# Tying first products to their places in the text on TensorE, and one more step ahead of the resized spectra's product

## The chip, the core and the metric

The kernel runs on one core of one Trainium2 chip. The core has five engines that run their own streams of instructions and meet through semaphores: TensorE (PE in the profile; its weight loads are PEld), VectorE (DVE), ScalarE (ACT), GpSimd (POOL) and SyncE (SP), which here only issues transfers. The metric is the device time of one execution in microseconds (us); lower is better.

## What is computed

Two layers are run one after the other on 32 images of 96 channels and 56 x 56 pixels, all in float32. Cut to what matters:

```python
# layer 0: expand, depthwise 3x3, squeeze and excite, project, residual
h = silu(bn(conv1x1(x, fake_quant(w1))))            # 96 -> 576 channels
h = silu(bn(depthwise3x3(h, fake_quant(w2))))
s = sigmoid(se_w2 @ silu(se_w1 @ mean(h) + b1) + b2)
x = x + bn(conv1x1(h * s, fake_quant(w3)))          # 576 -> 96

# layer 1
mag = abs(rfft2(x))                                 # first spectrum
fe  = mag.mean(channels)
ca  = sigmoid(mlp(pooled(separable_conv7(mag))))    # a gate for each channel
s   = [x.mean(channels), sqrt((x*x).mean(channels) + 1e-6), resize(fe)]
sa  = sigmoid(conv(relu(conv(separable_conv15(s)))))# a gate for each pixel
y   = x * ca * sa
freq_e = resize(abs(rfft2(y)).mean(channels))       # second spectrum
aux = [y, coord, freq_e]
offset, gate = conv3x3(aux), sigmoid(conv(relu(conv3x3(aux))))
y_def = deformable_conv3x3(y, offset)
z = (1 - gate) * conv3x3(y) + gate * y_def
x = relu(batchnorm(z) + x)                          # statistics over all images
```

A two-dimensional transform is done as two sets of matrix products, one along rows and one along columns, and the resize of its mean over channels as one more product.

## The kernel before

**Bands and slots.** The main loop (`layers`) goes over bands: 7 bands of 8 rows in each image. A band is cut into two halves of 7 tiles. A slot is one call of `pump()`: one for each of the 14 tiles and three at the end of a band, so 17 slots a band and 119 an image. The band's own work, in the text's order, is: the weights' loads for a coming half (`prepare`, on the SP queue), the joint convolution of the band after next (L605, in `find`), the products of three tiles (L721), three slots, the end of the previous half (its deformable product L740, the multiplication of loaded weights L692, the transposes L707 of a coming half with the copy L709), the products of four tiles, four slots, and the copies L732 that pack the half. The second half is the same; three slots close the band.

**Two streams beside it.** While the bands of image b run, `pump()` also advances two generators. The first does layer 0 of image b+2 (`hidden`: products L168, SiLU L172, nine depthwise taps L261 on VectorE, SiLU L221, a store of the result to `h2d` in memory). The second does `attend` for image b+1. Both start with the sixth band of an image (`turn`), and a generator runs from one `yield` to the next at each step. How many steps are due follows from the slot:

```python
            for st in streams:
                due = st[2] * min(1.0, (slot - st[3]) / (st[4] - st[3]))
                while st[1] < due:
                    st[1] += 1
                    next(st[0], None)
```

For the second stream `st[2]` is `n_second`, the number of its steps, which is counted while the first image is prepared: 61. With slots counted from the start of the stretch, `st[3]` is 3 and `st[4]` is 111, so that the 61 steps are spread evenly over 108 slots. One further piece, after the last `yield`, runs when the stretch is drained.

**The second stream's steps**, in order, which the change touches:

1. `squeeze` (L284, L290), with loads of `hq`, the stored hidden rows (`project_loads`, L305). Four rounds of `project` follow, four steps each. A round multiplies in two halves (L323, and L329 for the chunk that both share). `hq` has one buffer for each half, so a round's load starts when the products of the round before have read the buffer. ScalarE scales the result (L333), POOL adds the residual (L466) and stores it to `x1d` (L467).
2. `dft_mag` without a gate: three loads of `x2` (L361), then six groups (row products L386; squares L370 and copies L393 on ScalarE; sums L372 on VectorE; each group's step also issues the load three groups on), then three steps of column products (L410, with squares L413 on ScalarE and sums L414 on VectorE), then a root (L417).
3. `resized_spectrum` for `fe`: the reduction L427 on VectorE, a step's end, then the product L430 and a copy L432. After it come `edge` and the small products of the channel gate and the pixel gate (L501 to L556).
4. `dft_mag` with the pixel gate: the same, but POOL multiplies each group by the gate first (`weigh`, L366), two groups ahead. There are no squares L370 and no sums.
5. `resized_spectrum` for `fy`: multiplication L426, reduction L427, a step's end, L430 and L432; then L572, and at the drain the store of `fq`, which the next image's bands read.

**What sets the order.** SP issues its transfers exactly in the order of the text (`manual_schedule`). On the other engines a planner orders the instructions by its own estimate of when each is ready, with the text's order as the priority: an instruction can run ahead of earlier ones that the planner takes to be not ready. Once ordered, an engine works its instructions off one after the other. `keep_in_program_order` ties an instruction behind the one that the text emitted just before it on the same engine. The kernel uses it once, for ScalarE's L670.

**Buffers.** Products go to banks of `mm` (six, given out in turn by `bank`), `acc` (one) and `pd` (one). A bank comes free when its reader on ScalarE or VectorE is done. `sq`, `ht`, `ybl` and each half of `hq` have one buffer.

Of the kernel before, what the change touches and what calls it, by code (L numbers as in the profile page):

```python
# [16 lines left out]
C, H, W = 96, 56, 56  # L17
# [7 lines left out]
V = W // 2 + 1  # L25
# [8 lines left out]
EW = ER * W  # L34
# [67 lines left out]
def bn_affine(nc, pool, g, b, m, v, tag):  # L102

    shape = list(g.shape)
    std = pool.tile(shape, FP, name=f"std_{tag}")
    nc.vector.tensor_scalar(std, v, EPS, None, ALU.add)
    nc.scalar.activation(std, std, AF.Sqrt)  # L107
    nc.vector.reciprocal(std, std)
    inv = pool.tile(shape, FP, name=f"bninv_{tag}")
    nc.vector.tensor_tensor(inv, g, std, ALU.mult)  # L110
    sh = pool.tile(shape, FP, name=f"bnsh_{tag}")
    nc.vector.tensor_tensor(sh, m, inv, ALU.mult)
    nc.vector.tensor_tensor(sh, b, sh, ALU.subtract)
    return inv, sh


def bank(p):
    return p["mm"].tile([128, 512], FP, name="mm")


def hidden_constants(tc, ctx, a, p):

    nc = tc.nc
    cp = ctx.enter_context(tc.tile_pool(name="l0c", bufs=1))
    w = p["w0"] = {}
    for name, shape in (("w1", [C, HID]), ("w2", [128, NCH, 9]), ("w3", [128, NCH, C])):
        w[name] = cp.tile(shape, FP, name=name)
        nc.sync.dma_start(w[name], a[name + "L"])
    for name in ("sew1", "seb1", "sew2", "seb2"):
        w[name] = cp.tile(list(a[name].shape), FP, name=name)  # L130
        nc.scalar.dma_start(w[name], a[name])
    for name, parts in (("w1", C), ("w2", 128), ("w3", 128)):
        with tc.tile_pool(name=f"fq{name}", bufs=1) as tp:
            fake_quant(nc, tp, w[name], parts, name)
    with tc.tile_pool(name="l0v", bufs=1) as tp:
        vec = tp.tile([128, 8, NCH], FP, name="vec")
        nc.scalar.dma_start(vec, a["hidvec"])
        vec3 = tp.tile([C, 4], FP, name="vec3")
        nc.scalar.dma_start(vec3, a["bn3"])
        for n, v in ((1, vec[:, :4]), (2, vec[:, 4:]), (3, vec3.unsqueeze(2))):  # L140
            inv, sh = bn_affine(nc, tp, v[:, 0], v[:, 1], v[:, 2], v[:, 3], n)
            for key, t in ((f"inv{n}", inv), (f"sh{n}", sh)):
                w[key] = cp.tile(list(t.shape), FP, name=key)
                nc.vector.tensor_copy(w[key], t)

    p["hp"] = [cp.tile([128, HH + 2, WP], FP, name=f"hp{i}") for i in range(2)]
    for t in p["hp"]:
        nc.gpsimd.memset(t, 0.0)
    p["n_hp"] = 0
# [165 lines left out]
def project(nc, p, rows):  # L315

    w, w3s = p["w0"], p["w3scaled"]
    pts = []
    for half in range(2):
        pts.append(bank(p))  # L320
        mine = [(ch, hq) for ch, hq in rows[half] if ch < NCH - 1]
        for i, (ch, hq) in enumerate(mine):
            nc.tensor.matmul(pts[half][:C, :EW], w3s[:, ch], hq, start=(i == 0), stop=False)  # L323
        if half == 0:
            yield
    (_, both), = [r for r in rows[1] if r[0] == NCH - 1]
    for half in range(2):
        ps = slice(64 * half, 64 * half + 64)
        nc.tensor.matmul(pts[half][:C, :EW], w3s[ps, NCH - 1], both[ps], start=False, stop=True)  # L329
    outs = []  # L330
    for half in range(2):
        o = p["o"].tile([C, EW], FP, name="o")
        nc.scalar.activation(o, pts[half][:C, :EW], AF.Identity, bias=w["sh3"], scale=w["inv3"])  # L333
        outs.append(o)
    yield outs


def dft_mag(nc, p, src, gate=None):

    w = p["w"]
    hwc = src.rearrange("c (h w) -> h c w", h=H)
    s1 = p["s1p"].tile([2 * WX, NP, 2 * V], FP, name="s1")  # L350
    if gate is None:
        parts = p["sq"].tile([2 * WX, 2, NPB * V], FP, name="sq")[: 2 * H, :, : NG * W].rearrange("p k (g w) -> p k g w", g=NG)
    x2s = []

    def load(g):
        if g < NG:
            x2 = p["x2"][p["n_x2"] % len(p["x2"])]
            p["n_x2"] += 1
            for half in range(2):
                c0 = half * C // 2 + g * CG  # L360
                nc.sync.dma_start(x2[half * H : (half + 1) * H, :, :W], hwc[:, c0 : c0 + CG])  # L361
            x2s.append(x2)

    def weigh(g):
        if gate is not None and g < NG:
            nc.gpsimd.tensor_tensor(x2s[g][:, :, :W], x2s[g][:, :, :W], gate.unsqueeze(1).to_broadcast([2 * H, CG, W]), ALU.mult)  # L366

    def sums(g):
        sq = bank(p)[: 2 * H, : CG * W].rearrange("h (c w) -> h c w", c=CG)
        nc.scalar.activation(sq, x2s[g][:, :, :W], AF.Square)  # L370
        for k, t in enumerate((x2s[g][:, :, :W], sq)):
            nc.vector.tensor_reduce(parts[:, k, g], t.rearrange("h c w -> h w c"), AX.X, ALU.add)  # L372

    for g in range(3):
        load(g)
    for _ in range(2):
        yield
    weigh(0)
    weigh(1)
    yield  # L380
    if gate is not None:
        yield
    for g in range(NG):
        pt = bank(p)
        for i in range(CG // 2):
            nc.tensor.matmul(pt[:, i * 4 * V : (i + 1) * 4 * V],  # L386
                             x2s[g][:, 2 * i : 2 * i + 2, :].rearrange("h c w -> h (c w)"), w["FU"],
                             start=True, stop=True)
        if gate is None:
            sums(g)  # L390
        weigh(g + 2)
        load(g + 3)
        nc.scalar.copy(s1.rearrange("p (h q) u -> p h q u", h=2)[:, :, g * CG // 2 : (g + 1) * CG // 2],  # L393
                       pt[:, : 2 * CG * V].rearrange("p (q h u) -> p h q u", h=2, u=2 * V))
        yield
    if gate is None:
        p["sums"] = p["sp"].tile([2 * H, 2, W], FP, name="sums")
        nc.vector.tensor_reduce(p["sums"], parts.rearrange("p k g w -> p k w g"), AX.X, ALU.add)
    mag = s1[:, :, :V]
    n = NQB * V  # L400
    pairs = mag.rearrange("p (r q) u -> p r q u", r=2)
    for q0 in range(0, NP // 2, NQB):
        sq = p["sq"].tile([2 * WX, 2, 2, n], FP, name="sq")
        pts = bank(p), bank(p)
        for part, first, second in ((0, (0, 0), (1, V)), (1, (0, V), (2, 0))):
            for t, (g, u0) in enumerate((first, second)):
                for r, k in ((0, 0), (1, 1), (0, 1), (1, 0)):
                    rows = slice(r * WX, r * WX + W)
                    q1 = k * NP // 2 + q0
                    nc.tensor.matmul(pts[r][k * WX : (k + 1) * WX, part * n : (part + 1) * n].rearrange("p (q u) -> p q u", q=NQB),  # L410
                                     w["GV"][rows, g], s1[rows, q1 : q1 + NQB, u0 : u0 + V], start=(t == 0), stop=(t == 1))
        for r, pt in enumerate(pts):
            nc.scalar.activation(sq[:, r].rearrange("p k n -> p (k n)"), pt[:, : 2 * n], AF.Square)  # L413
        nc.vector.tensor_tensor(pairs[:, :, q0 : q0 + NQB], sq[:, :, 0].rearrange("p r (q u) -> p r q u", q=NQB),  # L414
                                sq[:, :, 1].rearrange("p r (q u) -> p r q u", q=NQB), ALU.add)
        yield
    nc.scalar.activation(mag, mag, AF.Sqrt)  # L417
    p["magnitude"] = mag


def resized_spectrum(nc, p, mag, name, scale=None):


    m2 = p["sp"].tile([2 * WX, V], FP, name=f"m_{name}")
    if scale is not None:
        nc.vector.tensor_tensor(mag, mag, scale.unsqueeze(2).to_broadcast([2 * WX, NP, V]), ALU.mult)  # L426
    nc.vector.tensor_reduce(m2, mag.rearrange("p q u -> p u q"), AX.X, ALU.add)  # L427
    yield
    pf = p["acc"].tile([128, 512], FP, name="acc")
    nc.tensor.matmul(pf[:V, : 2 * W], m2, p["w"]["RT2"], start=True, stop=True)  # L430
    rs = p["sp"].tile([V, 2, W], FP, name=name)
    nc.scalar.copy(rs.rearrange("p m w -> p (m w)"), pf[:V, : 2 * W])  # L432
    p["resized"] = rs
    yield


def attend(tc, p, b, x, h2d, pooled, x1, given=False):
# [32 lines left out]


    yield from dft_mag(nc, p, x1)
    mag = p["magnitude"]

# [89 lines left out]


    yield from dft_mag(nc, p, x1, sa)
    yield
    yield from resized_spectrum(nc, p, p["magnitude"], "fy", cx)
    fy = p["resized"]
    pz = p["acc"].tile([128, 512], FP, name="acc")  # L570
# [929 lines left out]
```

## Time and profile before

| | |
|---|---|
| three runs, us | 9,635.6, 9,640.8, 9,673.78; median 9,640.8 |
| the profiled execution, us | 9,648.5, of which its span is 9,646.7 |
| mean granted clock of TensorE | 0.923 of full speed |
| product L323, idle time before it | 127.4 us, of which 125.9 for hq |
| product L386, idle time before it | 52.4 us: 34.3 for POOL, 17.9 for x's loads |
| product L430 on fe's sums, idle time before it | 43.1 us |
| product L430 on fy's sums, idle time before it | 43.5 us |
| multiplication L692, idle time before it on VectorE | 704.2 us, of which 690.5 for the weights' loads |

The profile is of one execution. "Busy" is the time in which an engine works, "idle before" the time in which it stood still just before the instructions of a group, with what ended most of it (written after the arrow). The granted clock is what the chip's throttle allows TensorE; at 0.5 the same product takes about twice as long. The chain that ended last, which the page follows back from the end, lies in the last 280 us (`normalise`), where images are loaded, scaled and stored; the bands end at about 9,365 us.

### The profile page before, as it was taken

The page shows a single profiled execution, that of the slowest core. Times are in us where ns is not written, and L with a number is a line of the kernel's source. Part 1 is how long each engine was busy: PE and PEld are TensorE (multiplying, and loading weights), DVE is VectorE, ACT ScalarE, POOL GpSimd, SP SyncE. Part 2 cuts the span into 40 slices and gives each one's busy share as a digit, 9 for nine tenths or more (in the row PEclk, how much of TensorE's full clock was granted, in tenths as well). Part 3 has the DMA queues.
Part 4 walks back from the last instruction along what each step waited for, and adds up shares of the span by engine and source line. Part 5 has one row for each costly group of instructions (what it writes and reads, how often), then busy time and mean ns, then how long its engine had stood idle before and what let it go on. Part 6 is the DMA issues. An engine that isn't in the chain of part 4 may idle for free. (4 is left out here: it accounts for less than half of the span.)

```text
span 9646.7 us, 129705 instructions
## 1 busy us (share of the span) xinstructions
PE 8472.7 (88%) x48374; PEld 5064.2 (52%) x48374; DVE 7227.2 (75%) x6948; ACT 5322.1 (55%) x10262; POOL 2532.6 (26%) x2642
## 2 busy tenths in 40 slices
PE   6889989998999999999899989999999999999870
PEld 3455555555555555555555555555555555555540
DVE  7688777778777787877777887777878777777323
ACT  2355555565555556555555655555555555565453
POOL 1123223222222322222232322233222323322210
PEclk9899999999999999999999999999999999999985
DMA  2355555555555555555555555555555555554449
GB/s 94 95 143 148 151 152 160 150 149 143 147 155 154 160 154 145 145 149 155 154 160 155 145 142 153 151 158 154 153 139 145 150 157 157 153 152 135 130 154 417
DMA packets 1069473, 1485.98 MB, mean 154 GB/s; under 512 B 590438, under 2 KB 840086, under 8 KB 1056550
## 3 DMA queue, kind: packets, MB, share of 16 engines
q1 hardware_dynamic: 858747, 985.20, 37.9%
q10 hardware_dynamic: 153803, 329.80, 9.2%
q0 software_dynamic: 56288, 162.60, 6.7%
q8 instruction: 388, 6.36, 0.3%
q14 instruction: 247, 2.02, 0.1%
HBM read 1064.29 MB, written 412.65 MB: 153 GB/s over the span
## 5 line engine op out<-in xcount | busy, mean ns | idle before, releaser
L261 DVE SCALAR_TENSOR_TENSOR acch<-hp,w,acch 128x1512 f32<-128x1512 f32 (+1 forms) x2250 | 4320.5, 1920 | 32.8
L605 PE MATMUL mm<-yp,c_jointW 104*128 104x448 f32 x4032 | 1649.0, 561 | 9.0 <-ACT yt L709 5.5
L740 PE MATMUL pd<-v,c_def 128*96 128x224 f32 (+1 forms) x6272 | 1414.8, 376 | 127.6 <-ACT v L732 104.1
L703 POOL COPY ybl<-yp 96x448 f32<-96x448 f32 x896 | 1014.7, 1159 | 1903.7 <-PE mm L707 1903.3
L721 PE MATMUL mm<-wc,yt 64*96 64x144 f32 x12544 | 1168.1, 308 | 153.5 <-DVE yb L638 76.8
L740 PEld LDWEIGHTS pd<-v,c_def 128*96 128x96 f32 (+1 forms) x6272 | 1051.8, 173 | 437.4 <-ACT v L732 142.5
L168 PE MATMUL mm<-xt,w 96*128 96x392 f32 (+3 forms) x2688 | 1136.3, 561 | 133.8 <-ACT yt L709 96.0
L605 PEld LDWEIGHTS mm<-yp,c_jointW 104*128 104x128 f32 x4032 | 783.6, 196 | 806.0 <-issue 762.6
L721 PEld LDWEIGHTS mm<-wc,yt 64*96 64x96 f32 x12544 | 884.2, 167 | 489.8 <-issue 188.0
L221 ACT ACTIVATE acch<-acch,sh,inv 128x1568 f32<-128x1568 f32 x288 | 487.5, 1693 | 1159.0 <-DVE acch L261 1143.9
L692 DVE TENSOR_TENSOR wc<-wc,wr 128x1008 f32<-128x1008 f32 x448 | 564.6, 1260 | 704.2 <-DMA wr<-hd 690.5
L725 ACT COPY v<-mm 96x288 f32<-96x288 f32 (+1 forms) x2688 | 1003.6, 442 | 117.7 <-PE mm L721 78.9
L172 ACT ACTIVATE hp<-mm,sh,inv 128x392 f32<-128x392 f32 (+2 forms) x1216 | 811.8, 672 | 326.9 <-PE mm L168 282.1
L633 PE MATMUL mm<-yp,c_base0W 96*64 96x448 f32 x4032 | 913.5, 550 | 0.0
L323 PE MATMUL mm<-hq,w3s 128*96 128x392 f32 x2048 | 788.2, 531 | 127.4 <-DMA hq<-h2d 125.9
L655 POOL DMA_DIRECT2D od<-at x224 | 186.3, 832 | 2275.1 <-DVE at L651 1451.9
L732 ACT COPY v<-v 32x448 f32<-32x448 f32 x1344 | 755.3, 562 | 30.3
L168 PEld LDWEIGHTS mm<-xt,w 96*128 96x128 f32 (+1 forms) x2688 | 389.9, 189 | 495.1 <-issue 264.8
L709 ACT COPY yt<-mm 128x384 f32<-128x384 f32 (+1 forms) x896 | 350.9, 441 | 491.5 <-PE mm L707 489.4
L323 PEld LDWEIGHTS mm<-hq,w3s 128*96 128x96 f32 x2048 | 336.3, 173 | 477.7 <-issue 382.5
L466 POOL TENSOR_TENSOR o<-o,xc 96x392 f32<-96x392 f32 x256 | 396.5, 1549 | 643.9 <-ACT o L333 642.3
L633 PEld LDWEIGHTS mm<-yp,c_base0W 96*64 96x64 f32 x4032 | 294.6, 134 | 515.5 <-issue 490.2
(194 smaller groups left out, 9023.7 us busy)
## 6 DMA issues: line engine op xcount, KB each, us to landing
h2d<-acch ACTq DMA_DIRECT2D x288, 784.0 KB
wc<-hd SPq DMA_DIRECT2D x896, 252.0 KB
wr<-hd SPq DMA_DIRECT2D x896, 252.0 KB
hq<-h2d SPq DMA_DIRECT2D x128, 980.0 KB
hq<-h2d SPq DMA_DIRECT2D x128, 784.0 KB
x<-x1d SPq DMA_DIRECT2D x768, 98.0 KB
ht<-od SPq DMA_DIRECT2D x224, 252.0 KB
hd<-ht ACTq DMA_DIRECT2D x224, 252.0 KB
```

What stands on the lines that cost most here:

```text
L168: nc.tensor.matmul(pt[p0 : p0 + w1.shape[1], : rows * W], w1, xts[hf][:, r0 * W : (r0 + rows) * W], start=True, stop=True)
L172: nc.scalar.activation(h1[lo:hi, row0 : row0 + rows, 1 : 1 + W], pt[lo:hi, : rows * W].rearrange("p (h w) -> p h w", h=rows), AF.Silu, bia ...
L261: nc.vector.scalar_tensor_tensor(acc[:, lo:hi], win, wk, acc[:, lo:hi], ALU.mult, ALU.add)
L323: nc.tensor.matmul(pts[half][:C, :EW], w3s[:, ch], hq, start=(i == 0), stop=False)
L605: nc.tensor.matmul(view, weights[:, k], yp[:channels, r0 : r0 + RB, dx + PD - 1 : dx + PD - 1 + W], start=(k == 0), stop=(k == NTAP - 1))
L633: nc.tensor.matmul(pb[k % 2 * BC : (k % 2 + 1) * BC, :BW].rearrange("p (h w) -> p h w", h=RB), w["base"][:, k], yp[:C, r0 : r0 + RB, dx + ...
L692: nc.vector.tensor_tensor(wc, wc, wr, ALU.mult)
L703: nc.gpsimd.tensor_copy(yb[:, :, s], blocks)
L721: nc.tensor.matmul(pt[k][:C, (t - lo) * KP : (t - lo + 1) * KP], yt[ps, t], s[ps, t * KP : (t + 1) * KP], start=True, stop=True)
L725: nc.scalar.copy(v[:C, :, lo:hi, k].rearrange("c k t p -> c t k p"), pt[k][:C, : (hi - lo) * KP].rearrange("c (t k p) -> c t k p", t=hi - ...
L732: nc.scalar.copy(v[C:, 1 + 2 * i : 3 + 2 * i], v[i * QC : (i + 1) * QC, KA:])
L740: nc.tensor.matmul(out.rearrange("c q (t x) -> c t q x", x=TS), p["w"]["def"][ks, k], v[ks, k].rearrange("c t s (r x) -> c t (s r) x", r=T ...
```

## The change

Three first products are tied: the first of each half of `project` (L323), the first of each group of the second, gated row transform (L386) and the product of each resized spectrum (L430). The helper `pinned` makes the tie if the pools' dictionary holds the context, as it does in the main loop. In `resized_spectrum` one more `yield` stands between the reduction and the product, so that a step passes between them; it is met twice in an image.

```diff
+def pinned(p, ins):
+    if "tc" in p:
+        p["tc"].keep_in_program_order(ins)
+
@@ project
         for i, (ch, hq) in enumerate(mine):
-            nc.tensor.matmul(pts[half][:C, :EW], w3s[:, ch], hq, start=(i == 0), stop=False)
+            ins = nc.tensor.matmul(pts[half][:C, :EW], w3s[:, ch], hq, start=(i == 0), stop=False)
+            if i == 0:
+                pinned(p, ins)
@@ dft_mag
         for i in range(CG // 2):
-            nc.tensor.matmul(pt[:, i * 4 * V : (i + 1) * 4 * V],
-                             x2s[g][:, 2 * i : 2 * i + 2, :].rearrange("h c w -> h (c w)"), w["FU"],
-                             start=True, stop=True)
+            ins = nc.tensor.matmul(pt[:, i * 4 * V : (i + 1) * 4 * V],
+                                   x2s[g][:, 2 * i : 2 * i + 2, :].rearrange("h c w -> h (c w)"), w["FU"],
+                                   start=True, stop=True)
+            if i == 0 and gate is not None:
+                pinned(p, ins)
@@ resized_spectrum
     nc.vector.tensor_reduce(m2, mag.rearrange("p q u -> p u q"), AX.X, ALU.add)
     yield
+    yield
     pf = p["acc"].tile([128, 512], FP, name="acc")
-    nc.tensor.matmul(pf[:V, : 2 * W], m2, p["w"]["RT2"], start=True, stop=True)
+    pinned(p, nc.tensor.matmul(pf[:V, : 2 * W], m2, p["w"]["RT2"], start=True, stop=True))
```

`n_second` is counted from the generator itself and so counts the two new steps. Nothing else in the kernel is edited, and what is computed stays the same.

## The prediction

> **What bounds the kernel now.** I read the page first: how full each engine is, and the granted clock of TensorE (PE) by slice.
>
> ```profile
> PE 8472.7 (88%) x48374; PEld 5064.2 (52%) x48374; DVE 7227.2 (75%) x6948; ACT 5322.1 (55%) x10262; POOL 2532.6 (26%) x2642
> PEclk9899999999999999999999999999999999999985
> ```
>
> TensorE is busy for 8,364.6 of the 9,165 us from 200 to 9,365 us. The last 280 us are the normalisation, which the page's chain ends on and which the change does not touch. So what counts is where TensorE stands idle. That is the view of its waits; the columns are who waits, for whom, us in total, times, longest.
>
> ```profile
> PE mm L323 <- DMA hq<-h2d: 125.9, 31, 9.4
> PE mm L168 <- ACT yt L709: 96.0, 44, 5.2
> PE mm L707 <- ACT sq L413: 80.3, 21, 6.5
> PE acc L430 <- DVE m_fe L427: 43.1, 31, 4.2
> PE acc L430 <- DVE m_fy L427: 40.0, 30, 2.9
> PE mm L386 <- POOL x L366: 34.3, 32, 4.0
> ```
>
> Some 30 times each means once an image: the stalls sit at fixed places of an image's 119 slots. An image takes 282.7 us (L430 at 856.9 and 1,139.6 us), a slot 2.4 us. So the third view is the instructions in order of time of one image. Around the first L430:
>
> ```profile
> 4240.81 1.21 DVE L692 TENSOR_TENSOR wc<-wc,wr 128x1008 f32<-128x1008 f32 x1 [4.86 <-DMA wr<-hd]
> ...
> 4242.67 1.00 ACT L413 ACTIVATE sq<-mm 128x464 f32<-128x464 f32 x2 [4.73 <-DVE s L414]
> 4243.28 0.47 PE L707 MATMUL mm<-c_ident,ybl 96*128 96x96 f32 x3 [1.12 <-ACT sq L413]
> ...
> 4246.43 1.41 ACT L417 ACTIVATE s<-s 128x1392 f32<-128x1392 f32 x1
> 4247.74 0.77 ACT L709 COPY yt<-mm 128x384 f32<-128x384 f32 x2
> 4248.26 0.93 PE L168 MATMUL mm<-xt,w 96*128 96x392 f32 x2 [2.03 <-ACT yt L709]
> ...
> 4248.39 2.54 DVE L427 TENSOR_REDUCE m_fe<-s 128x29 f32<-128x1392 f32 x1
> ...
> 4251.09 0.55 PE L430 MATMUL acc<-c_RT,m_fe 128*29 128x112 f32 x2 [1.90 <-DVE m_fe L427]
> 4251.56 1.68 PE L168 MATMUL mm<-xt,w 96*128 96x392 f32 x2
> ```
>
> It is one knot. DVE waits 4.86 us for weights, so its L414 is late, so ScalarE's square L413 is late, so a bank is not free for L707; then the root L417 is late, the copy L709 behind it, and the reduction L427 ends 0.16 us before L430 starts. Three stalls of 5.05 us in all. The last row is a product pair that takes 0.93 us at 4,248.26 and 1.68 here: the clock has halved, from 4,249.5 to 4,256.3 us (third column before the end is the granted clock):
>
> ```profile
> 4249.50:4256.30 6.80, 5.21 (x9) 2.65 (x10) 6.80 (x7) 6.27 (x12) 0.00 (x0) 0.50 0.14 38
> ```
>
> **The three ties.** A tie makes a product issue after the one that the text emits just before it on TensorE; it adds no wait and does not hold what follows. I set the order in which the 25,755 products ran against the order in which the text emits them. L740 runs ahead of earlier emitted products 671 times, L721 437 times, L284 255 times; L323, L386 and L430 never. So every tied product already stands behind its neighbour, and the ties cost and bring 0. If a tie did hold, its product would start later: at best other products fill the 125.9 us that L323 waits, at worst what reads it is late too (ScalarE's L333 waits 60.1 us for L329 now). Ends -126 and +60; I take 0, by the count.
>
> **The added yield** is what acts. It is met twice an image, so n_second goes from 61 to 63. Step k runs in the first slot s with k-1 < N(s-3)/108.
> - Reduction of fe: k=35, 34*108/61+3=63.2, slot 64; after, 34*108/63+3=61.3, slot 62. Its product: slot 65 in both (k 36, then 37).
> - Multiply and reduction of fy: k=59, slot 106; after (k=60) 105. Its product: slot 108 in both.
> - The first three loads, L284 and L290, stay; from there to the first reduction steps come 0 to 2 slots earlier, between the two L430 and up to the second reduction again 0 to 2.
>
> Terms, against the profiled execution (9,648.5 us around a span of 9,646.7):
>
> A. L430's own waits, 43.1 + 40.0 us, 1.4 us each. The reductions get 4.8 and 2.4 us more. Taken: -75 (nine tenths); ends 0 and -83.
>
> B. Their neighbours. In the knot the transform's three L410 steps move from slots 57, 58, 60 to 55, 57, 58 and the root from 62 to 60. The second L414 then falls where the first was, ahead of the blocked L692. L707's 80.3 us and the 46.6 of L168 that stand in this knot sum to 126.9; three fifths, -76, ends -127 and +127 (a new knot as large). At fy, the last L410 step moves from slot 103 to 101, past the joint convolution L605 of the next band:
>
> ```profile
> 4332.64 7.02 PE L605 MATMUL mm<-yp,c_jointW 104*128 104x448 f32 x18
> ...
> 4340.50 1.86 PE L410 MATMUL mm<-s,c_GV 56*64 56x232 f32 x32
> ...
> 4345.34 1.28 ACT L417 ACT_TABLE_LOAD   x1
> ...
> 4352.78 0.38 PE L430 MATMUL acc<-c_RT,m_fy 128*29 128x112 f32 x2 [1.22 <-DVE m_fy L427]
> ```
>
> L410 goes 7 us earlier, and the root no longer stands in front of the copy L636. Of L721's waits for L638 38.9 us are there; half, -19, ends -39 and +39. B is -95.
>
> C. The clock. Before the end, half-speed stretches sum to 1,195 us, each costing half its length. 321 us of them begin within 7 us of the knot's stalls, 112 us around fy's. Half of 160 and of 56: -108, ends -216 and +108. [...]
>
> D. hq. The long wait, 30 times 4.2 us, is the first half of the fourth round (slot 32, then 31). Its load starts when the third round's first product frees the buffer; that moves from slot 25 to 24, ahead of L763 and 12 L721 (1.0 + 0.9 us). The load takes 13.0 us (4,148.0 to 4,161.0) behind five others. TensorE comes no earlier. Taken: half of 1.8 us 30 times, -25; ends -55 and, since the second half moves from slot 35 to 34 and so in front of an L605 of 7.0 us, +124 (rival 3).
>
> E. Second transform on POOL: groups 3 and 4 of L386 move from slots 94 and 96 to 93 and 94. Weighing L366 now ends 0.5 us late for group 3; the L168 (0.9 us) that ran before it now runs after: 0.9*31, +28, and 12 for group 4: +40; ends 0 and +124 (rival 2).
>
> F. Elsewhere. 45 steps move; the stalls of moved steps (124.9 + 126.9 + 19.7) are 6 us a step. Some ten move two slots or past an L605 and may meet a new stall: +60, ends 0 and +150. SP keeps its order but for x and hq loads that come a slot earlier relative to weights; those loads wait for TensorE and free SP sooner, taken as 0.
>
> Sum: -75 - 95 - 108 - 25 + 40 + 60 = -203. DVE waits 690.5 us for weights and the change leaves that, so a TensorE that runs ahead meets the next late DVE result; I let three fifths through: -122, 9,526.5. The profiled execution is 7.7 us above the median of the three runs, so **9,520 us** against 9,640.8 (-1.25%).
>
> **Rivals.**
> 1. *Hidden anyway.* Only A comes, at three fifths (-45), and F takes some of it back (+15): 9,611. For it: every stall's next neighbour waits for DVE. Against: the knot hangs on the steps that move. 18 in 100.
> 2. *POOL takes over, slower.* Group 4 of the second transform now stands in front of the L740 at 4,313.8 us. Its weighing queues behind a store of zd that waits for DVE, and ends at about 4,317.8 (start 4,316.35, 2.92 us for two). TensorE then waits 4.0 us, 31 times 124, and half a 3.4 us stretch of slow clock, 53: less A's 45, 9,773. It decides if weighing ends over 2 us after the 12 L721. Against: L740 is one of the products that pass a late L386. 13 in 100.
> 3. *hq takes over, slower.* The second half of round four, before L605 at about 4,166 us, finds its load (issued 4,157.1) still under way. At 11 us to landing it waits 2 us: 62 + 53 - 45, 9,711. It decides from 9 us. Against: the queue's packets of this size end by 4,163. 9 in 100.
>
> **How the numbers follow.** The forecast has 60 in 100; its own range is 9,430 (all of B's and C's gains, nothing of F) to 9,592. The range of all reaches to rivals 1 and 3 and leaves out rival 2 and some 6 in 100 below: 9,400 to 9,730. No change that can be told is within 0.5%, 48 us. Faster 60, same 18, slower 22.
>
> **What would show it.** L430's two waits under 10 us together: A right. L707 on L413 below 30 us and half-speed stretches below 1,050 us: B and C right. L323's wait near 100 us; if it is gone, the ties do act and my reading of them is wrong. L386 on POOL over 100 us is rival 2, L323 over 180 us rival 3. If L430's waits go and the span does not fall, rival 1.

## The result, and the profile after

The changed kernel takes 9,893.0 us (median of four runs, 9,886.3 to 9,895.7) against 9,650.3 for the kernel before on the same chip: 1.024 times as long, with an interval of 1.022 to 1.026. The prediction had said 1.25% faster.

The lines of the new kernel stand 5 to 10 further down: L707 is L717 now, L721 is L731, L692 is L702, L414 is L423, L417 is L426, L430 is L440, L323 is L328, L386 is L393, L740 is L750. In the kernels of the experiments they move by a few more lines; each name is that of the kernel it is read from. The page, engines and granted clock:

```profile
PE 8551.9 (87%) x48374; PEld 5116.9 (52%) x48374; DVE 7242.9 (73%) x6948; ACT 5370.7 (54%) x10292; POOL 2599.7 (26%) x2642
PEclk9889999999899999999999999999999999998985
```

TensorE runs the same 48,374 instructions and is busy for 79 us more, so they ran at a slower clock (mean granted clock 0.910, 0.923 before); ScalarE has 30 instructions more, all of them loads of its function table. Who TensorE waits for (us in total, times, longest):

```profile
PE mm L393 <- POOL x L373: 125.3, 58, 3.6
PE mm L731 <- DVE yb L648: 122.9, 73, 5.2
PE mm L717 <- ACT gate L764: 122.2, 15, 9.2
PE mm L328 <- DMA hq<-h2d: 103.8, 30, 10.1
...
PE mm L328 <- issue: 95.1, 15, 8.3
PE mm L717 <- ACT v L735: 91.9, 14, 6.9
...
PE mm L731 <- ACT hp L177: 57.3, 74, 2.3
...
PE acc L440 <- ACT v L735: 0.6, 1, 0.6
```

What was to go has gone: L430's 83.1 us (0.6 now), L707's 80.3 on the square, L168's 96.0 on L709. What has come is larger: 214.1 us of L717 on ScalarE at the very slot of the old knot (for the gate in 15 images, for the copy in the 14 between them), 95.1 of L328 on "issue" (nothing that the profile shows) in every second image, and 91.0 more of L393 on POOL.

The knot now, in order of time (the same image that the prediction showed):

```profile
4325.44 0.64 DVE L423 TENSOR_TENSOR s<-sq 128x464 f32<-128x464 f32 x1 [2.10 <-ACT sq L422]
...
4326.18 1.01 ACT L422 ACTIVATE sq<-mm 128x464 f32<-128x464 f32 x2
...
4327.07 0.63 ACT L764 ACTIVATE gate<-mm,halves 96x448 f32<-96x448 f32 x1
...
4327.72 1.28 ACT L426 ACT_TABLE_LOAD   x1
...
4328.70 2.81 PE L750 MATMUL pd<-v,c_def 96*96 96x224 f32 x14
...
4333.61 1.21 DVE L702 TENSOR_TENSOR wc<-wc,wr 128x1008 f32<-128x1008 f32 x1 [7.52 <-DMA wr<-hd]
...
4335.68 0.64 DVE L423 TENSOR_TENSOR s<-sq 128x464 f32<-128x464 f32 x1
4336.35 1.40 ACT L426 ACTIVATE s<-s 128x1392 f32<-128x1392 f32 x1 [7.35 <-DVE s L423]
4337.77 1.28 ACT L764 ACT_TABLE_LOAD   x1
...
4339.06 0.63 ACT L764 ACTIVATE gate<-mm,halves 96x448 f32<-96x448 f32 x1
4339.60 0.92 ACT L735 COPY v<-mm 96x432 f32<-96x432 f32 x2
...
4339.84 1.35 PE L717 MATMUL mm<-c_ident,ybl 96*128 96x96 f32 x7 [8.32 <-ACT gate L764]
```

Read it from DVE. The spectrum's squares are summed in three parts; the second sum still runs in time, at 4,325.4. The last square is ready at 4,327.2 us, but DVE has gone on to an L702 that the text emits only in slot 71, thirteen slots after the sum; its loads end at 4,333.6, and the sum L423 stands behind it until 4,335.7. The root L426 needs that sum, and it now stands further ahead on ScalarE: in front of the second gate L764 and the copies L735, which empty the banks that L717 is to write. In the kernel before, both gates and the copies of this place ran before the root:

```profile
4235.97 1.15 ACT L754 ACTIVATE gate<-mm,halves 96x448 f32<-96x448 f32 x2
4237.00 0.94 ACT L725 COPY v<-mm 96x432 f32<-96x432 f32 x2
...
4246.43 1.41 ACT L417 ACTIVATE s<-s 128x1392 f32<-128x1392 f32 x1
```

Now TensorE has run dry at 4,331.5 and stands for 8.32 us. The windows of this stretch (length, busy time and instructions by engine, then the granted clock, DMA share, GB/s) show what comes with it; the second one is at half speed throughout:

```profile
4323.00:4336.00 13.00, 8.52 (x81) 5.37 (x74) 3.38 (x5) 5.85 (x10) 0.00 (x0) 1.00 0.54 146
4336.00:4353.00 17.00, 11.56 (x34) 6.94 (x35) 15.22 (x17) 14.98 (x26) 1.06 (x2) 0.50 0.06 15
```

The second new wait has the same look. At the tenth slot of the stretch, before:

```profile
4104.59 0.17 DVE L292 TENSOR_TENSOR s<-acc,seb 128x5 f32<-128x5 f32 x1 [3.65 <-PE acc L290]
4105.03 0.17 DVE L294 TENSOR_SCALAR s<-s 128x5 f32<-128x5 f32 x1 [0.27 <-ACT s L293]
4105.23 0.66 DVE L296 TENSOR_TENSOR w3s<-w,s 128x480 f32<-128x480 f32 x1
4109.41 1.21 DVE L692 TENSOR_TENSOR wc<-wc,wr 128x1008 f32<-128x1008 f32 x1 [3.52 <-DMA wr<-hd]
```

and after:

```profile
4185.83 0.17 DVE L297 TENSOR_TENSOR s<-acc,seb 128x5 f32<-128x5 f32 x1 [3.65 <-PE acc L295]
4186.03 0.21 ACT L298 ACTIVATE s<-s 128x5 f32<-128x5 f32 x1 [0.34 <-DVE s L297]
...
4193.03 1.21 DVE L702 TENSOR_TENSOR wc<-wc,wr 128x1008 f32<-128x1008 f32 x1 [7.03 <-DMA wr<-hd]
4194.15 0.17 DVE L299 TENSOR_SCALAR s<-s 128x5 f32<-128x5 f32 x1
4194.35 0.66 DVE L301 TENSOR_TENSOR w3s<-w,s 128x480 f32<-128x480 f32 x1
...
4195.11 4.97 PE L328 MATMUL mm<-hq,w3s 128*96 128x392 f32 x8 [6.87 <-issue]
```

The multiplication of the weights has slipped in between the squeeze's first and second instruction; the 0.83 us of work behind it waits for 7 us, and L328 starts 0.10 us after the last of it. Before, DVE waited here too, for 3.52 us, but the squeeze was done by then.

### The profile page after: what moved, and what is told of

It is laid out like the page before. It is cut to its first block, busy times and chain, and to the rows that moved or that the text cites. A ratio compares the mean times of both kernels' runs of the same rounds, so it can differ in the third digit from the quotient of the medians.

```text
span 9884.4 us, 129917 instructions
## 1 busy us (share of the span) xinstructions
PE 8551.9 (87%) x48374; PEld 5116.9 (52%) x48374; DVE 7242.9 (73%) x6948; ACT 5370.7 (54%) x10292; POOL 2599.7 (26%) x2642
## 5 line engine op out<-in xcount | busy, mean ns | idle before, releaser
L713 POOL COPY ybl<-yp 96x448 f32<-96x448 f32 x896 | 1093.5, 1247 | 2449.6 <-PE mm L717 2449.6
L750 PE MATMUL pd<-v,c_def 128*96 128x224 f32 (+1 forms) x6272 | 1479.4, 385 | 126.9 <-ACT v L742 99.2
L731 PE MATMUL mm<-wc,yt 64*96 64x144 f32 x12544 | 1216.2, 311 | 226.6 <-DVE yb L648 122.9
L750 PEld LDWEIGHTS pd<-v,c_def 128*96 128x96 f32 (+1 forms) x6272 | 1080.4, 178 | 478.8 <-ACT v L742 134.2
L731 PEld LDWEIGHTS mm<-wc,yt 64*96 64x96 f32 x12544 | 926.2, 170 | 574.5 <-issue 219.9
L702 DVE TENSOR_TENSOR wc<-wc,wr 128x1008 f32<-128x1008 f32 x448 | 553.5, 1236 | 780.1 <-DMA wr<-hd 768.6
L735 ACT COPY v<-mm 96x288 f32<-96x288 f32 (+1 forms) x2688 | 1004.0, 441 | 198.6 <-PE mm L731 156.0
L328 PE MATMUL mm<-hq,w3s 128*96 128x392 f32 x2048 | 815.1, 546 | 206.4 <-DMA hq<-h2d 103.8
L328 PEld LDWEIGHTS mm<-hq,w3s 128*96 128x96 f32 x2048 | 358.3, 180 | 587.7 <-issue 458.0
L635 ACT ACTIVATE hid<-mm,c_dg1b 50x448 f32<-50x448 f32 x224 | 140.8, 628 | 811.2 <-PE mm L615 795.0
L393 PE MATMUL mm<-c_FU,x 112*128 112x116 f32 x3072 | 454.4, 297 | 142.5 <-POOL x L373 125.3
```

Source lines behind the costliest of these rows:

```text
L328: ins = nc.tensor.matmul(pts[half][:C, :EW], w3s[:, ch], hq, start=(i == 0), stop=False)
L702: nc.vector.tensor_tensor(wc, wc, wr, ALU.mult)
L713: nc.gpsimd.tensor_copy(yb[:, :, s], blocks)
L731: nc.tensor.matmul(pt[k][:C, (t - lo) * KP : (t - lo + 1) * KP], yt[ps, t], s[ps, t * KP : (t + 1) * KP], start=True, stop=True)
L735: nc.scalar.copy(v[:C, :, lo:hi, k].rearrange("c k t p -> c t k p"), pt[k][:C, : (hi - lo) * KP].rearrange("c (t k p) -> c t k p", t=hi - ...
L750: nc.tensor.matmul(out.rearrange("c q (t x) -> c t q x", x=TS), p["w"]["def"][ks, k], v[ks, k].rearrange("c t s (r x) -> c t (s r) x", r=T ...
```

## The experiments

Ratios are to the kernel before on the same chip, with 95% intervals. "Half speed" is the sum of the stretches at half clock up to TensorE's last product of the bands; "DVE for weights" is DVE's wait for the loads of the weights' multiplication (L692 before). The last four columns are us of the profiled execution.

| run | us | ratio | last product | PE idle | half speed | DVE for weights |
|---|---|---|---|---|---|---|
| before | 9,650.3 | 1 | 9,358 | 885 | 1,195 | 690.5 |
| changed | 9,893.0 | 1.024 [1.022, 1.026] | 9,595 | 1,043 | 1,485 | 768.6 |
| after_tie692 | 9,582.8 | 0.993 [0.991, 0.995] | 9,290 | 790 | 1,246 | 404.2 |
| before_tie692 | 9,462.7 | 0.981 [0.979, 0.983] | 9,166 | 778 | 1,045 | 386.8 |
| after_hold | 9,383.9 | 0.973 [0.971, 0.976] | 9,087 | 683 | 935 | 340.6 |
| before_hold | 9,396.1 | 0.973 [0.970, 0.976] | 9,109 | 748 | 918 | 397.9 |
| yields_hold | 9,355.4 | 0.967 [0.965, 0.969] | 9,065 | 684 | 915 | 326.4 |

**Which part of the change does it.** Four kernels take the change apart.

yields_only turns the ties off:

```diff
 def pinned(p, ins):
-    if "tc" in p:
-        p["tc"].keep_in_program_order(ins)
+    return
```

> The change without its three ties: only the added yield, met twice an image, is left. Theory (the yield does it all: the ties change the order of 519 of TensorE's products and hold nothing that matters): 9,860 to 9,930 us, as the changed kernel, with L717's waits for ScalarE's gate and copy (122 and 92 us there) and L328's 95 us on issue still there under their own lines. Rival (the tie on the resized spectrum's product holds the products behind it back, and that is the cost): 9,500 to 9,700 us.

Measured: 9,832.5 us, 1.0175 [1.0153, 1.0197], with L717 (L716 there) 124.2 and 92.4 us on gate and copy and L328 (L327 there) 101.9 on issue. The yield makes about three quarters of the loss, 1.75 of 2.4%. The ties are not free beside it: some 0.6%.

ties_only keeps the ties and has one `yield`, as before.

> The kernel before with the three ties and without the added yield. Theory (every tied product already stands behind its neighbour in the text): 9,620 to 9,680 us, no difference. Rival (the ties cost by themselves): over 9,700 us.

Measured: 9,668.3 us, 1.0002 [0.9989, 1.0015]. The order of instructions in this kernel is that of the kernel before on every engine: by themselves the ties move nothing, as predicted.

yield_before moves the extra yield:

```diff
+    yield
     m2 = p["sp"].tile([2 * WX, V], FP, name=f"m_{name}")
...
     yield
-    yield
     pf = p["acc"].tile([128, 512], FP, name="acc")
```

> The changed kernel with the extra yield put ahead of the reduction L427 rather than behind it. The second stream still has 63 steps an image, so all earlier steps fall into the same slots as in the changed kernel, but the reduction and its product are one step apart as before. Theory (the pace of 63 steps is what costs; the room between reduction and product is worth its own 80 us of waits and no more): 9,860 to 9,990 us, the waits of L717 and L328 there, some of L430's 80 us back. Rival (the reduction taken ahead of other work of DVE is the cost): 9,600 to 9,720 us.

Measured: 9,885.5 us, 1.0222 [1.0202, 1.0242]; L717 124.6 and 92.1, L328 101.9 on issue. The pace does it. One part of the expectation missed: L440's waits did not come back, they sum to 1.1 us. So it was the pace that removed them too.

reduce_early gives the product the same room at the old pace:

```diff
     nc.scalar.mul(s3[:, 0], pm[:H, :W], 1.0 / C)
-    yield
...
     yield from dft_mag(nc, p, x1, sa)
-    yield
...
     nc.vector.tensor_reduce(m2, mag.rearrange("p q u -> p u q"), AX.X, ALU.add)
     yield
+    yield
```

> The kernel before with two yields between reduction and product but the yield ahead of the reduction taken out, so that the reduction is made in the step of the root L417. The stream still has 61 steps: no other step moves. Theory (room between reduction and product saves L430's 83 us of waits, and nothing else goes wrong while the pace is as before): 9,540 to 9,640 us, L430 under 10 us, L707's 80 us on the square and L168's 96 us on L709 still there. Rival (an early reduction delays DVE's weights and squares behind it): over 9,690 us.

Measured: 9,658.9 us, 1.0002 [0.9988, 1.0015], and L430 (L431 there) still waits for 84.6 us. Neither theory: the reduction did not come earlier. In order of time:

```profile
4250.04 1.41 ACT L417 ACTIVATE s<-s 128x1392 f32<-128x1392 f32 x1
...
4252.01 2.55 DVE L427 TENSOR_REDUCE m_fe<-s 128x29 f32<-128x1392 f32 x1
...
4254.70 0.55 PE L431 MATMUL acc<-c_RT,m_fe 128*29 128x112 f32 x2 [1.16 <-DVE m_fe L427]
```

The reduction follows the root by 0.56 us, whatever step it is emitted in. The wait was the root's lateness: room for the reduction does not help while the root stays where it is.

product_late leaves all as it was before and emits fe's product (alone) one step later, by exchanging the `yield` behind it for one ahead of it.

> The kernel before with the product of fe alone put one step later, ahead of the step that follows it: no step added, the pace of 61 as before, and all else in its place. Theory (room behind the reduction takes L430's own wait away for fe, 41 us, and no more): L430 on m_fe under 5 us, m_fy as before, 9,580 to 9,640 us. Rival (the wait moves to what follows): 9,640 to 9,690, no difference. Of the whole change this is the part that was meant without the shift of the other steps.

Measured: 9,635.6 us, 0.9987 [0.9975, 1.0000]; L430 on fe 43.1 to 4.7 us. So a later product removes the wait as an earlier root does, but of its 38 us only some 12 arrive, at the edge of what can be told.

**Is it DVE's place for the weights?** The tie used by the change itself, now on the multiplication:

```diff
-    nc.vector.tensor_tensor(wc, wc, wr, ALU.mult)
+    p["tc"].keep_in_program_order(p["tc"].nc.vector.tensor_tensor(wc, wc, wr, ALU.mult))
```

> The changed kernel with DVE's multiplication of the weights (L702, wc and wr) tied to its place in the text, so that DVE no longer takes it ahead of other work while its loads are on the way. Theory (the new waits of L717 at the knot, 214 us, and of L328 on issue, 95 us, both come from DVE standing at L702 with the square's sum L423 or the squeeze behind it): both go, L717 under 60 us in all and L328 on issue under 20, and with half of the clock loss the time falls to 9,550 to 9,680 us. Rival (the waits come from ScalarE's order, the root and its table loads ahead of gate and copy, whatever DVE does): L717 stays above 150 us and the time above 9,800.

> The control: the kernel before with the same tie on the weights' multiplication, L692 there. Theory (the knot of before hangs on DVE's wait at L692): L707's 80 us on the square go, L168's 47 us behind it too, and the time falls by 100 to 200 us, to 9,460 to 9,560. Rival (the tie makes the weights late and TensorE waits for them instead): slower than 9,700.

Measured: 9,582.8 and 9,462.7 us, so 3.1% and 1.9% less. The changed kernel's waits with the tie:

```profile
PE mm L328 <- issue: 94.4, 14, 8.3
...
PE mm L717 <- ACT gate L764: 14.7, 15, 1.0
```

The root still stands ahead of gate and copies there, and L717 loses 14.7 us rather than 214.1. So ScalarE's order alone costs little: it hurts only when the root's input is late, and that is DVE's doing. L707's wait in the kernel before went as well. But L328 kept its 94 us, and 120 us still lay between the two. In the trace L702 still stood ahead of L299 and L301: a tie puts an instruction behind the one emitted just before it on its engine, here a statistics instruction that itself runs early, and not behind all earlier ones.

To test that, the multiplication was emitted four slots later (after_wlate, before_wlate: out of the middle of a half, to just ahead of `pack`, tied).

> The changed kernel with the weights' multiplication tied as in after_tie692 and also emitted four slots later in the text, at the end of a half, so that its loads have landed when DVE comes to it. Theory (L328's 94 us on issue, which the tie alone left, come from the same wait: DVE stands 7 us at L702 with the squeeze's L299 and L301 behind it): L328 on issue under 20 us, and 9,420 to 9,530 us against the 9,583 of after_tie692. Rival (L328 at that place waits for something else, such as the hq loads behind the weights' loads on SP's queue): L328 stays above 80 us and the time above 9,560.

> The control on the kernel before, tied and four slots later too. Theory (at the pace of 61 the tie alone has already taken the knot; some of DVE's waits at L692 are left): 9,400 to 9,470 us against the 9,463 of before_tie692. If the shift of the steps by itself costs nothing once DVE no longer waits for weights, this and after_wlate lie within 1% of each other; if it costs by itself, after_wlate stays 80 us or more above.

Measured: 9,666.5 us, 1.0008 [0.9991, 1.0025], and 9,754.6, 1.0098 [1.0064, 1.0133]. L328's wait on issue went, as the theory said, but against it the time rose in both, by 84 and 292 us over the tie alone. TensorE waits for the weights now, at the first products of a half. In the kernel before with this edit:

```profile
4646.03 1.18 DVE L692 TENSOR_TENSOR wc<-wc,wr 128x1008 f32<-128x1008 f32 x1
...
4647.31 1.37 PE L721 MATMUL mm<-wc,yt 64*96 64x144 f32 x8 [5.44 <-issue]
```

DVE's own wait for the loads fell to 218 us, less than in any faster kernel of the table, and L721's on issue rose from 6.3 in the kernel before to 230.1.

So the place in the text was right, and only the passing had to go. after_hold and before_hold leave it there and hold it behind the last twelve instructions of DVE:

```diff
+    old = [i for i in nc.cur_bb.bb.instructions[-400:] if i is not ins.ins and i.engine == ins.ins.engine]
+    for i in old[-HOLD:]:
+        tc.add_manual_dep(ins.ins, i.name, mybir.DependencyInfo(mybir.DependencyClass.NoSync, mybir.DependencyReason.DATA),
+                          reason="behind")
```

> The changed kernel with the weights' multiplication held behind the twelve instructions of DVE emitted before it, in place of the one of after_tie692, where L702 still stood ahead of the squeeze's L299 and L301; its place in the text and its loads stay. Theory (L328's 94 us come from DVE standing at L702 with the squeeze behind it): L328 on issue under 20 us, and 9,440 to 9,540 us against the 9,583 of after_tie692. Rival (the squeeze is late in any case): L328 above 70 us, 9,560 or more.

> The control: the kernel before, held the same way. Theory (there the squeeze's products stood a slot later, behind 20 products that cover it): little beyond the 9,463 of before_tie692, 9,400 to 9,480 us. The distance from after_hold is what the shift of the steps costs when DVE's wait for weights is out of it: under 60 us if that wait was the whole cause, over 80 us if not.

Measured: 9,383.9 us, 0.9731 [0.9705, 0.9757], and 9,396.1, 0.9729 [0.9702, 0.9756]. L328 on issue is gone, both are faster than expected, and they are equal within the intervals. They get there by different waits: L430's own 104.7 us stay in before_hold and are all but gone in after_hold (1.4), which waits 152.2 us for POOL's weighing where before_hold waits 43.3. The knot in after_hold:

```profile
4130.71 1.01 ACT L423 ACTIVATE sq<-mm 128x464 f32<-128x464 f32 x2
...
4131.75 0.64 DVE L424 TENSOR_TENSOR s<-sq 128x464 f32<-128x464 f32 x1
...
4133.54 1.41 ACT L427 ACTIVATE s<-s 128x1392 f32<-128x1392 f32 x1
...
4137.04 0.78 PE L723 MATMUL mm<-c_ident,ybl 96*128 96x96 f32 x7 [0.99 <-ACT gate L770]
```

The sum follows its square, the root follows its table load, and TensorE stands for 0.99 us in place of 8.32. DVE comes to the multiplication of slot 71 at 4,159.8, without a wait.

**Pace or places.** fe_only has the added yield for `fe` alone, 62 steps.

> The change with the added yield for fe alone: 62 steps an image rather than 63. From the order of the program: L328 of the first round stands in slot 10 ahead of the deformable products, as with 63 steps; at the knot both sums of squares stand behind DVE's multiplication of the weights, but the root stands behind gate and copies as before. Theory (each shift is read off in that way): L328 on issue 80 to 110 us, L717's waits on the gate gone and those on the square 80 to 200 us, 9,760 to 9,880 us. Rival (half of the yields, half of the cost, whatever the places): 9,730 to 9,760 us with the same lines at half their size.

Measured: 9,630.5 us, 0.9971 [0.9957, 0.9986]: a gain, against both. L328 stood in slot 10, as read, but without a wait: with 62 steps the planner leaves L299 and L301 ahead of the multiplication, which the expectation had not taken in. At the knot L718 (L717 in the changed kernel) waits 57.6 us on the square. The cost goes with who stands behind DVE's wait, not with the number of steps.

**POOL.** after_store9 emits the store of zd two slots later (`slot + 9`); the planner put it back, all engines ran the changed kernel's order, and 9,874.5 us, 1.0227 [1.0205, 1.0248], is that kernel once more.

> The changed kernel with the store of zd put two slots later in POOL's text (slot + 9 instead of slot + 7), so that it is issued behind the weighing of group 4. Theory (the store waits 3 us for DVE's z and holds the weighing): L393's wait for POOL falls from 125 us to 50 or less, and the time by 60 to 130 us, to 9,760 to 9,840. Rival (POOL's chain is late anyway, or DVE is the next in line): the wait moves, and the time stays above 9,870.

after_store20t takes 20 slots and ties the store, which puts it behind the weighings.

> The changed kernel with the store of zd 20 slots after its product instead of 7 and tied, so that on POOL it stands behind the weighings of groups 3 and 4 (with 9 slots, in after_store9, the planner had put it back in the very same order, and that run was one of the changed kernel again). Theory (the store's wait of 3 us for DVE's z holds the weighing): L393's wait for POOL falls from 125 us to 50 or less and the time by 50 to 120 us, to 9,770 to 9,850. Rival (something else is late at the same place): the wait moves to another line and the time stays above 9,870.

Measured: 9,883.8 us, 1.0233 [1.0202, 1.0263]. L393's wait falls from 125.3 to 51.6 us, and others rise: L717's on the copy from 91.9 to 117.4, L328's on hq from 103.8 to 120.6, L731's on hp from 57.3 to 75.6. after_hold_store does the same without the knot:

> after_hold with the store of zd 20 slots late and tied, as in after_store20t. There the store's wait went and the time stayed, since the knot lay behind it. Theory (with the knot gone, the part of L394's 152 us on POOL that the store makes counts): L394 on POOL under 120 us, 9,310 to 9,370 us, the fastest of all. Rival (another engine's lateness lies behind POOL again): the wait moves and the time stays at 9,375 to 9,400.

Measured: 9,392.0 us, 0.9719 [0.9705, 0.9732], as after_hold. L394's wait for POOL's weighing (L393's in the changed kernel) falls from 152.2 to 123.2, but 28.1 us of the same product for POOL's copy ybl come in its place, so TensorE waits for POOL as long as before; this kernel does not tell what a shorter wait would be worth. The rival is right both times in the time; only after_store20t shows it with the wait really gone.

**The tie on the resized product.** after_free430 drops it and keeps the two others; yields_hold drops all three and holds the weights.

> The changed kernel without the tie on the resized spectrum's product; the two other ties stay. Theory (of the 0.6% that lies between the changed kernel and the one without ties, all comes from this tie, which puts L440 of fe behind other products): 9,800 to 9,860 us, as without any tie. Rival (the ties on hq or on the groups' products hold, or the difference is chance): 9,870 to 9,910.

> The changed kernel without its three ties, with the weights' multiplication held as in after_hold. Theory (the tie on the resized spectrum's product cost 55 to 75 us only because it put products of the knot in a worse order; with the knot gone the ties are worth little): 9,350 to 9,400 us, within 0.4% of after_hold. Rival (the tie costs its 0.6% by itself): 9,300 to 9,340.

Measured: 9,818.9 us, 1.0160 [1.0128, 1.0191], and 9,355.4, 0.9670 [0.9647, 0.9693]. after_free430 has the order of yields_only on every engine, so the two other ties move nothing, and the tie on L430 makes the 0.6%. With the weights held, the kernel without ties is faster by about as much (0.967 against after_hold's 0.973, measured on two chips; on one chip, 0.967 against after_hold_store's 0.972), so it isn't the knot that makes the tie dear. The wait of the sampling products on hp (L737, L736) is 73.0 us in after_hold and 38.0 in yields_hold, but TensorE's idle time in all is the same, 683 and 684. How the tie costs stays open.

**Two parts together.** best is before_tie692 with product_late.

> Two of the tried parts together on the kernel before, at its pace of 61: the weights' multiplication tied as in before_tie692, and the product of fe one step later as in product_late. Theory (with the knot gone nothing behind fe's product is late, so its 63 us of waits now count): 9,390 to 9,440 us. Rival (they are given back further on, as in product_late): 9,450 to 9,475.

Measured: 9,472.7 us, 0.9813 [0.9789, 0.9837], as before_tie692. L432 (L430 before) still waits 58.5 us on fe: TensorE's order differs from that of before_tie692 in only five places, so in nearly every image the planner put the product back, and this run does not test the theory.

The fastest kernel tried is yields_hold: the extra step, no ties, the weights held.

## Why the prediction was wrong

- **A (L430's own waits, -75): right in size, not quite in cause.** They went from 83.1 to 0.6 us. The text gave the credit to the room behind the reduction ("The reductions get 4.8 and 2.4 us more"). In reduce_early that room without an earlier root left 84.6 us; in yield_before the earlier root without that room left 1.1.
- **B (the knot, -76; fy, -19): the step that failed.** "The second L414 then falls where the first was, ahead of the blocked L692." That is so, and the old waits of L707 and L168 went. But an image has three such sums; the last still stood behind the blocked multiplication, and the root, which needs all three, had moved ahead of gate and copies on ScalarE. L717 waits 214.1 us in place of the 126.9 of L707 and L168: the term is +87 in waits where -76 was taken. The bound of +127, "a new knot as large", was in the text without a place. At fy the term came, and more: L721's waits on yb near fy's product fell from 38.9 to 13.2 us. But the same line rose at two other places of the image, from 24.7 to 74.5 us some 220 us behind fe's product and from 11.6 to 35.3 some 56 us behind it, so that in all it is up by 46.1. With the weights held the second of these is gone, and 64.8 us of the first stay.
- **C (clock, -108): the right link, with B's sign.** Half speed rose from 1,195 to 1,485 us, and fell to 935 in after_hold, where the stalls went. At the old knot the 6.83 us at half speed followed gaps of at most 2.03 us. Of its three stalls, those of 1.1 and 2.0 us lie ahead of the fall at 4,249.5; the one of 1.9 us lies almost wholly in the slow stretch.
- **D (hq, -25): right in size.** L323 on hq fell by 22.1 us, and by 22.3 between the held kernels. That it is the load's earlier start was not tested.
- **E (POOL, +40) and rival 2: the wait right, its price not.** L393 on POOL rose by 91.0 us, to 125.3, over the 100 that the text gave as rival 2's sign and toward its priced 124. after_store20t, the one kernel that lowered TensorE's wait for POOL, left the time where it was: what is saved there is waited for elsewhere.
- **F (elsewhere, +60): too small.** L328 on issue alone is 95.1 us, and L731 on yb up by 46.1. The text said that L284 and L290 stay, and looked no further: L323 of the first round moved one slot, in front of the 20-odd products that had covered it, and DVE's multiplication slipped in between the squeeze's instructions.
- **The ties as 0: right** on the kernel before, where they move no instruction; with the yield L430's tie costs 0.6%, and the count was made on the order before the yield.
- **The three fifths.** "DVE waits 690.5 us for weights and the change leaves that": the wait's length was taken as given (it did rise by 78.1 only). What mattered was who stands behind it. Before, L692 ran ahead of earlier emitted instructions of DVE 234 times in 448, after 278 times; held behind them, never, and both kernels take some 9,390 us, 0.9731 and 0.9729. So the passing is what made the change slow. The change as it stands, shift and ties, is then worth nothing; the shift without the ties (yields_hold, 0.967) is worth some half a percent, which L430's tie takes back.
- **The range.** Its low end does not follow from its words: with all of B's and C's gains and nothing of F the terms sum to -442, three fifths of which is -265, or 9,376 us and not 9,430. The result lies far on the other side.

## What to carry to other kernels

When steps move, write down for every engine with a long wait which instructions stand behind the waiting one in the new order, and follow each to TensorE; the wait's own length tells little (the runs with the least of it at DVE were slower than the held ones). If an instruction that waits for a load runs ahead of work that is ready, hold it behind that work before tuning anything around it: here this was worth 2.7% in the kernel before and about 5% in the changed one, and made the change under study neutral. It is not the same as making the multiplication later: four slots later in the text cost 84 and 292 us. A stall that ends in "issue" can be a late VectorE result, as L328's 6.87 us were, whose input L301 ended 0.10 us before: look for what ended just before it.

## What the runs showed of the hardware

The 8.32 us stall of TensorE at the new knot came with 17.07 us at half clock, which set in 4.4 us into the stall and lasted 13.2 us beyond it; the smaller stalls of the old knot came with 6.83 us. So the clock made the new knot dearer than its waits say. Over the whole change TensorE stood idle for 158 us more and was busy for 79 us more with the same instructions.

Counted from the clock in the two traces: up to the last product of the bands, the kernel before has 165 half-speed stretches, 1,195 us in all: 57 of 3.41 us (the length that rivals 2 and 3 of the prediction reckon with), 59 of 6.83, 27 of 10.24 and 22 of 13.65 to 20.48. The changed kernel's has 179, 1,485 us in all: 48, 69, 26 and 36 of these lengths. A product of L605 took 954 ns in the median at half clock and 542 at full.

In the 3.41 us ahead of each of the 165 falls in the kernel before, TensorE was busy for 37% of the time in the median. Cut back from the falls into pieces of the same length, the other full-speed time of the bands from 100 us on gives 2,193, and TensorE was busy for at least 42% of each; but so it was ahead of 58 of the falls. At the old knot it was busy for 1.07 of the last 3.42 us, with a longest gap of 2.03.
